# Cross-attention and quantised FFN on one core: the loads of the first batch's tokens and context issued by ScalarE instead of SyncE

## The chip, the cores and the metric

The kernel runs on one core of one Trainium2 chip. The metric is the device time of one execution in microseconds (us), the median of the runs made. Engines are named as the profile names them: PE (TensorE matmul), PEld (its weight loads), DVE (VectorE), ACT (ScalarE), POOL (GpSimd) and SP (SyncE). SP computes nothing: it issues DMAs, and "SPq" in a profile line is SP at work on an issue.

## The reference

For 8 batches of 512 tokens of width 512, a layer norm of the tokens attends to 64 context rows per batch, the result is added to the tokens, and a feed-forward layer with quantised activations and ternary weights (hidden width 2048) is added to that. Cut to what matters:

```python
def xattn(xn, mem, mask):                       # xn = layernorm(x)
    scores = einsum('bsd,bmd->bsm', xn, mem) / sqrt(D)
    attn = softmax(where(mask[:, None, :], scores, -1e30))
    return where(any(mask), einsum('bsm,bmd->bsd', attn, mem), 0)

def linear_bit(x, w, g):
    xq = act_quant(rmsnorm(x, g))               # 8 bits, one scale per row
    wq = round(tanh(w / mean(abs(w)))) * arctanh(mean(abs(w)))
    return einsum('bsd,od->bso', xq, wq)

x = x + xattn(layernorm(x), ctx, mask)
y = layernorm(x)
x = x + linear_bit(silu(linear_bit(y, w1, g1)) * linear_bit(y, w2, g2), w3, g3)
```

Each of the three weight matrices is 4 MB. Its quantisation needs the mean of its absolute values first, so all of a matrix has to be in the chip before any of it can be used.

## The kernel before

All work is recorded as operations (`op(engine, cost, run, writes, reads)`) and then emitted in an order that is stored in the kernel as a packed list, `ORDER`. The costs given to `op` are those of a planner that made the list; the list is fixed, and the costs are not read when the kernel is built. Each engine does its own instructions in the order in which they were emitted, and waits where an operand is not there yet. SP issues every DMA of this kernel in the same way, one after the other. Eight semaphores tell of the landings of DMAs and are used in turn, so the issue of a DMA also waits until the DMA eight places before it in the order has landed.

The tokens of a batch are one tile `x` of 128 partitions, 4 rows of 512 numbers each (`c` = 0 to 3); the context of a batch is loaded twice into one tile `mem`, into partitions 0 to 63 and 64 to 127, 128 KB each. For two batches at a time the context also goes into a tile `both`, from which only a power-of-two scale per batch is taken. `load_x(b)` records these loads: `both` (L473, even batches only), two halves of `mem` (L478), and `x` (L485), which for batch 0 comes in two pieces of 512 KB (`c` = 0 and 1, then 2 and 3) and for the others in one of 1024 KB. `load_w(i)` records four loads of 1024 KB of a weight matrix (L322 and L326, tile `raw`).

The order of the first DMAs on SP is: the mask (L276, 64 KB), `both` (256 KB), the first half of `mem`, the first piece of `x`, the second half of `mem`, the second piece of `x`, then the four pieces of the first weight matrix, and then gains and further weights.

What the first loads feed, each on its engine in this order:

- DVE: unpacks the mask (`keep`, L281); takes the largest number of each row of `both` (`measure_mem`, L494), then of the columns after a transpose on PE (L502), limits and rounds it (L506, L513), and after a broadcast on PE (L517) makes the scales (L519 to L524, tile `mf`). Then come statistics of the first two rows of `x` (L560, L562), the low part of the split context (`split_mem`, L536, which reads `mem`, `mf` and ACT's high part), statistics of the other two rows of `x` (L560, L562) and shifts (L573).
- ACT: a load of its function table, the high part of the split context (L533, reads `mem` and `mf`), a copy (L310), one normalised row of `x` (L582), and then sums of absolute weights (`measure_w`, L353, reads `raw`), one line for each piece of the matrix.
- POOL: variances and inverse roots of them (L567, L291), normalised rows (`t`, L586), their low parts (`xh`, L592), later one half and more of the quantisation of weights (`tq`, L386).

After some 80 us all three weight matrices are quantised and transposed, and the matmuls of the eight batches run one after the other on PE to the end.

Of the kernel before, what the change touches and what calls it, by code (L numbers as in the profile page):

```python
# [59 lines left out]
PE, DVE, ACT, POOL, DMA = "PE", "DVE", "ACT", "POOL", "DMA"  # L60
# [27 lines left out]
class Plan:  # L88
# [19 lines left out]
    def op(self, engine, cost, run, writes, reads, table=None, other=()):  # L108

        me = len(self.ops)
        deps = set()
        pair = lambda x: x if isinstance(x, tuple) else (x, None)
        meets = lambda a, b: a is None or b is None or a == b
        for b, part in map(pair, reads):
            deps.update(o for q, o in b.writes if meets(part, q))
            b.reads.append((part, me))
            b.ops.append(me)
        for b, part in map(pair, writes):  # L120
            deps.update(o for q, o in b.writes + b.reads if meets(part, q) and o != me)
            b.writes.append((part, me))
            b.ops.append(me)
        tiles = {id(b): b for b, _ in map(pair, [*writes, *reads])}.values()
        self.ops.append(Op([(engine, cost, run), *other], deps, [b for b in tiles if b.tag], table))
        return me
# [72 lines left out]
def kernel(  # L199
# [15 lines left out]
    M = mem.shape[1]  # L215
    H = w1.shape[0]
    NC = S // P
# [16 lines left out]
    V, A, G, T, Q = nc.vector, nc.scalar, nc.gpsimd, nc.tensor, nc.sync  # L234
    plan = Plan()
    op = plan.op
# [4 lines left out]
    def few(name, n, key, dtype=F32, bufs=6):  # L241
        return plan.buffer(small, name, [P, n], dtype, bufs, f"{name}_{key}", bound=False)
# [226 lines left out]
    def load_x(b):  # L469
        if b % 2 == 0:  # L470
            both = plan.buffer(att, "both", [P, D], F32, BOTH, f"both_{b}")
            op(DMA, (475, 650, 729),
               lambda: Q.dma_start(both(), mem[b : b + 2].rearrange("b m d -> (b m) d")), [both], [])  # L473
            mem_f[b] = mem_f[b + 1] = measure_mem(b, both)
        mt = plan.buffer(att, "mem", [P, D], F32, 2, f"mem_{b}")
        for half in range(2):
            op(DMA, (475, 650, 364, 500),
               lambda half=half: Q.dma_start(mt()[half * M : (half + 1) * M, :], mem[b]),  # L478
               [(mt, half)], [])
        xt = plan.buffer(big, "big", [P, NC, D], F32, BIG, f"x_{b}")  # L480
        view = x[b].rearrange("(p c) d -> p c d", c=NC)
        n = 2 if b == 0 else NC
        for c in range(0, NC, n):
            op(DMA, (475, 650, 2750 * n // NC, 1400),
               lambda c=c: Q.dma_start(xt()[:, c : c + n, :], view[:, c : c + n, :]),  # L485
               [(xt, c + i) for i in range(n)], [])
        mts[b], xs[b] = mt, xt

    def measure_mem(b, both):


        f = few("mf", 7, b)
        op(DVE, 673,
           lambda: V.tensor_reduce(  # L494
               f()[:, 0:1], both(), AX.X, ALU.max, apply_absolute_value=True), [(f, 0)], [both])
        pr = plan.buffer(ps_a, "a", [1, 2, M], F32, 1, f"pam_{b}")
        op(PE, 110,
           lambda: T.transpose(pr().rearrange("p b m -> p (b m)"), f()[:, 0:1], ident()),
           [pr], [(f, 0), ident])
        tops = few("top", 2, b, bufs=2)  # L500
        top = lambda: tops()[0:1, :]
        op(DVE, 270, lambda: V.tensor_reduce(top(), pr(), AX.X, ALU.max), [tops], [pr])  # L502
        def limit():
            for i in range(2):
                one = tops()[0:1, i : i + 1]
                V.tensor_scalar(one, one, 2e-38, None, ALU.max)  # L506

        op(DVE, 209, limit, [tops], [])

        def power():  # L510
            for i in range(2):
                one = tops()[0:1, i : i + 1].bitcast(I32)
                V.tensor_scalar(one, one, 0x7F800000, None, ALU.bitwise_and)  # L513

        op(DVE, 209, power, [tops], [])
        pe = plan.buffer(ps_a, "a", [P, 2], F32, 1, f"pe_{b}")
        op(PE, 110, lambda: T.matmul(pe(), ones(), top(), start=True, stop=True),  # L517
           [pe], [ones, tops])
        op(DVE, 150, lambda: V.reciprocal(f()[:, 1:3], pe()), [(f, 1)], [pe])  # L519
        op(DVE, 150,  # L520
           lambda: V.tensor_scalar(f()[:, 3:5], pe(), float(D) ** -0.5, None, ALU.mult),
           [(f, 2)], [pe])
        op(DVE, 70,
           lambda: V.tensor_tensor(f()[:, 5:7], pe(), valid()[:, b : b + 2], ALU.mult),  # L524
           [(f, 3)], [pe, valid])
        return f
# [487 lines left out]
    constants()  # L1014
    masks()
    load_x(0)
    load_w(0)
    for g, src in enumerate((g1, g2)):
# [11 lines left out]
    for c in range(AHEAD):  # L1030
        for j in range(NW):
            gate(0, c, j)
    whole(quantise_w(1))
    load_x(1)
    load_w(2)
    whole(measure_w(2))
# [16 lines left out]
    def during(b):  # L1053

        t = 4 * NC * b
        if b == 0:
            job(t, t + 3, quantise_w(2))
            job(t + 0, t + 4, pre(1), expo(1))
            job(t + 5, t + 6, post(1))
            z = quantise_x(1)  # L1060
            job(t + 7, t + 11, half(z)), job(t + 12, t + 15, half(z))
            job(t + 6, t + 6, once(load_x, 2))
            job(t + 10, t + 10, once(load_x, 3))
            job(t + 12, t + 15, pre(2))
            return
        if b + 1 < B:
            z = quantise_x(b + 1)
            job(t, t + 3, expo(b + 1), post(b + 1))
            job(t + 4, t + 7, half(z)), job(t + 12, t + 15, half(z))
        if b + 2 < B:  # L1070
            job(t + 8, t + 15, pre(b + 2))
        if b + 3 < B:
            job(t + 3, t + 3, once(load_x, b + 3))
# [70 lines left out]
```

## Time and profile before

| what | value |
|---|---|
| median of 3 runs | 428.0 us (427.61 to 428.92) |
| the profiled execution | 427.9 us, of which its span is 425.8 us |
| busy, share of the span | PE 91%, DVE 87%, POOL 87%, ACT 80% |
| PE busy, 0 to 80 us | 47.7 us |
| PE busy, 110 to 420 us | 309.8 of 310 us |
| DMA queue of the program | one (q1), 66.93 MB |

A line of the profile's groups gives the source line, the engine, the operation, what it writes and reads, and a count. A line of the timeline gives start and duration in us, the engine (SPq for SP's issues), the source line, the operation, `out<-in`, and in square brackets how long the engine sat idle before it and what ended that. "DMA to landing" is the time from the start of an issue until the semaphore told that all bytes had arrived. The view by stretches gives, for each stretch, its length, the busy time of each engine with the number of instructions, the granted clock of PE, the mean busy share of the 16 DMA engines and the rate of the data.

### The profile page before, as it was taken

How to read it: one execution, taken by the hardware profiler on the slowest of the kernel's cores; microseconds unless marked ns; L12 is line 12 of the kernel's file. 1: busy time of each engine (PE TensorE's matmuls, PEld its weight loads, DVE VectorE, ACT ScalarE, POOL GpSimd, SP SyncE). 2: the span in 40 equal slices, each digit the busy share in tenths (PEclk: the TensorE clock that was granted, in tenths of full speed). 3: DMA queues.
4: the chain of work that ended last, by engine and by line, in shares of the span. 5: the costliest groups of instructions: out<-in, count | busy, mean ns of one | idle time of the engine just before them, and what ended most of it. 6: DMA issues, size and time to landing. Idle time of an engine off the chain costs nothing.

```text
span 425.8 us, 6677 instructions
## 1 busy us (share of the span) xinstructions
PE 388.8 (91%) x2174; PEld 192.8 (45%) x2174; DVE 369.0 (87%) x832; ACT 341.3 (80%) x464; POOL 368.7 (87%) x330
## 2 busy tenths in 40 slices
PE   0563878999999999999999999999999999999996
PEld 0341534544444544454445444544454444444444
DVE  4689999999998998799989998999789888897772
ACT  1799999979899799598996898988686986774531
POOL 1789998998999999699999999999699979988650
PEclk9996899999999999999999999999999999999999
DMA  7999994497555578863589635864644546533272
GB/s 217 408 406 376 380 208 52 103 255 147 126 112 150 99 131 157 183 174 68 104 158 276 136 76 82 171 174 83 134 76 148 75 87 146 152 77 73 49 207 90
DMA packets 142514, 67.35 MB, mean 158 GB/s; under 512 B 133136, under 2 KB 133520, under 8 KB 140048
## 3 DMA queue, kind: packets, MB, share of 16 engines
q1 hardware_dynamic: 142480, 66.93, 63.4%
q8 instruction: 17, 0.28, 0.3%
q14 instruction: 17, 0.14, 0.1%
HBM read 25.76 MB, written 8.39 MB: 80 GB/s over the span
## 4 chain that ended last, share of the span: by engine, by line
PE 78%; DVE 6%; POOL 6%; DMA 3%; issue 3%; ACT 2%; SPq 0%; DVEq 0%; POOLq 0%; ACTq 0%
PE p L883 48%; PE pd L825 24%; PE po L683 3%; DMA zT<-xm 2%; PE psc L602 2%; POOL tq L386 2%; DVE st L560 1%; DMA both<-in_ctx_dram 1%; PE pd L854 1%; POOL t L586 1%; POOL xh L592 1%; POOL mv L291 1%; DVE zf L741 1%; DVE h L927 1%; ACT h L899 1%
## 5 line engine op out<-in xcount | busy, mean ns | idle before, releaser
L883 PEld LDWEIGHTS <-zT 128*128 128x128 f16 x1024 | 99.5, 98 | 122.0 <-issue 3.0
L940 POOL TENSOR_TENSOR h<-h,g_bc 128x1024 f32<-128x1024 f32 x55 | 130.4, 2377 | 2.7 <-ACT sq L932 2.1
L883 PE MATMUL p<-w1T,zT 128*128 128x512 f16 x512 | 120.4, 383 | 2.4 <-DVE zT L309 1.5
L883 PE MATMUL p<-w2T,zT 128*128 128x512 f16 x512 | 119.2, 379 | 1.1 <-DVE h L927 0.9
L825 PE MATMUL pd<-w3T,hT 128*128 128x512 f16 x496 | 117.8, 379 | 0.0
L927 DVE SCALAR_TENSOR_TENSOR h<-p,zf,h 128x1024 f32<-128x1024 f32 x64 | 81.9, 1280 | 14.9 <-PE p L883 8.4
L899 ACT ACTIVATE h<-p,zf 128x1024 f32<-128x1024 f32 x64 | 70.1, 1105 | 24.8 <-PE p L883 17.0
L932 ACT ACTIVATE sq<-h 128x1024 f16<-128x1024 f32 x64 | 67.2, 1050 | 17.0 <-DVE h L927 14.8
L825 PEld LDWEIGHTS <-hT 128*128 128x128 f16 x496 | 47.9, 98 | 55.6 <-DMA hT<-h 0.2
L964 DVE TENSOR_REDUCE hf<-h 128x1 f32<-128x2048 f32 x31 | 70.6, 2278 | 1.8 <-POOL h L940 1.7
L736 POOL TENSOR_TENSOR z<-xm,g_bc 128x1024 f32<-128x1024 f32 x29 | 69.8, 2423 | 1.4 <-ACT xm L725 0.6
L997 ACT ACTIVATE h<-h,hf 128x2048 f16<-128x2048 f32 x23 | 45.8, 1994 | 0.2 <-DVE hf L968 0.2
L741 DVE TENSOR_REDUCE zf<-z 128x2 f32<-128x1024 f32 x32 | 38.8, 1211 | 5.8 <-POOL z L736 5.7
L592 POOL TENSOR_TENSOR xh<-t,xh 128x512 f16<-128x512 f32 x32 | 37.3, 1168 | 2.0 <-DVE xh L591 1.2
L799 ACT ACTIVATE xm<-z,zf 128x512 f16<-128x512 f32 x42 | 28.1, 709 | 0.7 <-DVE zf L760 0.7
L731 ACT ACTIVATE xsq<-x,xf 128x512 f32<-128x512 f32 x32 | 22.9, 715 | 6.5 <-DVE x L691 6.0
L835 DVE SCALAR_TENSOR_TENSOR x<-pd,hf,x 128x512 f32<-128x512 f32 x31 | 23.1, 744 | 3.0 <-PE pd L825 2.6
L691 DVE SCALAR_TENSOR_TENSOR x<-po,mx,x 128x512 f32<-128x512 f32 x32 | 22.9, 745 | 1.3 <-PE po L683 1.2
L602 PE MATMUL psc<-mT,xT 128*128 128x128 f16 x256 | 19.7, 224 | 1.9 <-DMA xT<-xh 1.9
L560 DVE BATCH_NORM_STATS2 st<-x 128x6 f32<-128x512 f32 x32 | 21.3, 679 | 0.0
L602 PEld LDWEIGHTS <-xT 128*128 128x128 f16 x256 | 16.9, 101 | 8.5 <-DMA xT<-xh 3.5
L291 POOL TENSOR_TENSOR hf<-hf,neg_half 128x1 f32<-128x1 f32 x32 | 20.1, 634 | 0.2
(134 smaller groups left out, 483.4 us busy)
## 6 DMA issues: line engine op xcount, KB each, us to landing
raw<-in_L_ffn_w_dram SPq DMA_DIRECT2D x10, 1024.0 KB, 13.8
x<-in_x_dram SPq DMA_DIRECT2D x7, 1024.0 KB, 6.9
out_dram<-x SPq DMA_DIRECT2D x7, 1024.0 KB, 4.1
mem<-in_ctx_dram SPq DMA_DIRECT2D x16, 128.0 KB, 6.5
w3T<-in_L_ffn_w_dram SPq DMA_DIRECT2D x2, 1024.0 KB, 12.6
both<-in_ctx_dram SPq DMA_DIRECT2D x4, 256.0 KB, 8.2
x<-in_x_dram SPq DMA_DIRECT2D x2, 512.0 KB, 6.1
g_bc<-in_L_ffn_g_dram SPq DMA_DIRECT2D x1, 1024.0 KB, 14.9
```

Source lines behind the costliest of these rows:

```text
L592: rest = lambda e, t=t, xh=xh: e.tensor_tensor(xh()[:, 1, :], t(), xh()[:, 0, :], ALU.subtract)
L602: T.matmul(psc()[:, c, :, :].rearrange("p s m -> p (s m)"), xT()[:, k, :], mT().rearrange("p (s d) m -> p d s m", s=2)[:, k % ND, :, :], s ...
L736: gain = lambda e, xm=xm, z=z: e.tensor_tensor(z(), xm().broadcast_to([P, 2, D]), g_bc(), ALU.mult)
L741: lambda i=i, z=z, am=am: V.tensor_reduce(am()[:, i, :], z(), AX.X, ALU.max, apply_absolute_value=True),
L825: T.matmul(po(), hT()[:, n * P : (n + 1) * P], w3T()[:, n, :], start=(n == 0), stop=(n == NH - 1),)
L883: T.matmul(ps()[:, k * HC : (k + 1) * HC], zT()[:, g * ND + d, :], weight(d, j * HW // HC + k), start=(d == 0), stop=(d == ND - 1),)
L899: lambda: A.activation(h()[:, j * HW : (j + 1) * HW], ps(), AF.Silu, scale=fac()[:, 0:1]),
L927: lambda: V.scalar_tensor_tensor(cols(), ps(), fac()[:, 1:2], cols(), ALU.mult, ALU.mult),
L932: lambda: A.activation(sq(), cols(), AF.Square, scale=(RMS / H) ** 0.5, accum_out=col(j)),
L940: run = lambda e: e.tensor_tensor(cols(), cols(), g3_bc()[:, j * HW : (j + 1) * HW], ALU.mult)
L964: lambda: V.tensor_reduce(col(2), h(), AX.X, ALU.max, apply_absolute_value=True),
L997: op(ACT, 1995, lambda: A.activation(hq(), h(), AF.Copy, scale=col(5)), [h], [(f, 5)], other=[(POOL, 1970, lambda: G.tensor_scalar(hq(), h ...
```

## The change

In `load_x`, for batch 0 alone, the four loads of `mem` and `x` are issued by `nc.scalar` (`A`, ACT) instead of `nc.sync` (`Q`, SP). The load of `both` stays on SP, and so do all loads of other batches. The stored order is the same, so SP goes from `both` straight to the first weight piece, and ACT's first four instructions are the two halves of `mem` and the two pieces of `x`, in the order that they had. The changed planner costs (60 for 475) have no effect on the stored order.

```diff
+        queue = A if b == 0 else Q
         mt = plan.buffer(att, "mem", [P, D], F32, 2, f"mem_{b}")
         for half in range(2):
-            op(DMA, (475, 650, 364, 500),
-               lambda half=half: Q.dma_start(mt()[half * M : (half + 1) * M, :], mem[b]),
+            op(DMA, (60 if b == 0 else 475, 650, 364, 500),
+               lambda half=half: queue.dma_start(mt()[half * M : (half + 1) * M, :], mem[b]),
                [(mt, half)], [])
...
         for c in range(0, NC, n):
-            op(DMA, (475, 650, 2750 * n // NC, 1400),
-               lambda c=c: Q.dma_start(xt()[:, c : c + n, :], view[:, c : c + n, :]),
+            op(DMA, (60 if b == 0 else 475, 650, 2750 * n // NC, 1400),
+               lambda c=c: queue.dma_start(xt()[:, c : c + n, :], view[:, c : c + n, :]),
                [(xt, c + i) for i in range(n)], [])
```

## The prediction

> **What bounds the kernel now.** I read the page first: PE is busy 91% of the span. The view by stretches then says where PE is not the bound: from 110 to 420 us it is busy 309.8 of 310 us, from 0 to 80 us only 47.7 of 80. After 80 us the time is PE's own, so the change can only move the moment at which PE's steady stretch begins. Next come the stretches of the start:
>
> ```profile
> core 0: us, PE busy (x) PEld busy (x) DVE busy (x) ACT busy (x) POOL busy (x), PEclk, DMA share, GB/s
> 0.00:2.00 2.00, 0.00 (x0) 0.00 (x0) 0.54 (x4) 0.00 (x0) 0.69 (x6) 1.00 0.02 6
> 2.00:4.00 2.00, 0.00 (x0) 0.00 (x0) 0.05 (x1) 0.00 (x0) 0.00 (x0) 1.00 0.50 174
> 4.00:6.00 2.00, 0.04 (x1) 0.07 (x1) 1.25 (x3) 0.00 (x0) 0.00 (x0) 1.00 1.02 250
> 6.00:8.00 2.00, 0.85 (x3) 0.51 (x3) 1.30 (x7) 0.00 (x0) 0.00 (x0) 1.00 0.98 252
> 8.00:10.00 2.00, 0.04 (x1) 0.00 (x0) 1.70 (x7) 1.45 (x2) 0.13 (x1) 1.00 0.97 340
> 10.00:12.00 2.00, 0.78 (x8) 0.46 (x8) 1.42 (x3) 0.73 (x2) 0.79 (x2) 1.00 1.05 408
> ```
>
> The DMA engines are half idle from 2 to 4 us, and fully busy at only 250 GB/s while `x` and `mem` arrive, against 408 GB/s with weights. In the order of time the chain that ended last begins with the load of `both` (1.18 to 5.11 us), then DVE's work on it, then POOL. The timelines show who waits:
>
> ```profile
> 1.18 0.42 SPq L473 DMA_DIRECT2D both<-in_ctx_dram  x1
> 1.64 0.56 SPq L478 DMA_DIRECT2D mem<-in_ctx_dram  x1
> 2.24 0.57 SPq L485 DMA_DIRECT2D x<-in_x_dram  x1
> 2.86 0.47 SPq L478 DMA_DIRECT2D mem<-in_ctx_dram  x1
> 3.38 0.59 SPq L485 DMA_DIRECT2D x<-in_x_dram  x1
> 4.00 5.33 SPq L322 DMA_DIRECT2D raw<-in_L_ffn_w_dram  x4
> ...
> 8.53 1.28 ACT L533 ACT_TABLE_LOAD   x1 [8.53 <-DMA mem<-in_ctx_dram]
> 9.83 0.72 ACT L533 ACTIVATE ms<-mem,mf 128x512 f16<-128x512 f32 x1
> ...
> 8.22 0.15 DVE L524 TENSOR_TENSOR mf<-pe,valid 128x2 f32<-128x2 f32 x1
> 8.29 1.28 DVE L560 BATCH_NORM_STATS2 st<-x 128x6 f32<-128x512 f32 x2
> 9.48 0.30 DVE L562 BATCH_NORM_AGGREGATE mv<-st 128x2 f32<-128x6 f32 x2
> 10.58 0.75 DVE L536 SCALAR_TENSOR_TENSOR ms<-mem,mf,ms 128x512 f16<-128x512 f32 x1 [0.80 <-ACT ms L533]
> 11.25 1.28 DVE L560 BATCH_NORM_STATS2 st<-x 128x6 f32<-128x512 f32 x2
> ...
> 13.02 0.19 POOL L567 TENSOR_SCALAR mv<-mv 128x2 f32<-128x2 f32 x1 [2.14 <-DVE mv L562]
> ```
>
> To be seen: ACT's table load waits for `mem` alone (in the trace the wait for its two halves stands ahead of it; the scale `mf`, ready at 8.25 us, is waited for only by the ACTIVATE behind it). Those 1.28 us come after the landing of `mem`, then ACT's 0.72 us, and DVE sits 0.80 us for it. POOL waits 2.14 us for DVE's second statistics. So the start has two chains: `both` to DVE, and the second half of `mem` to ACT to DVE. Landings, from the issues of these tiles: `mem` takes 3.9 and 5.6 us, so its halves land at 5.5 and 8.4; `x` 5.8 and 6.5, so at 8.0 and 9.8; the first weight piece 8.4, at 12.4.
>
> **The change part by part.** *Four issues leave SP.* They take 0.56 + 0.57 + 0.47 + 0.59 = 2.19 us; the first weight piece is issued at 1.64 instead of 4.00. The third and fourth pieces still wait, by the semaphores used in turn, for the mask (ready for DVE at 3.95) and `both`. *Four issues join ACT.* No row shows ACT issuing; taken at SP's durations with SP's gaps of 0.05 us, and begun at 0.72 like SP's first, they end near 3.1. ACT's first other work stands at 8.53, so 5.4 us cover them; at twice the price they would still end at 5.4. Cost 0; without cover, 2.2.
>
> *`mem` and `x` are issued 0.9 to 1.0 us earlier* (`mem` at 0.72 and 1.94, `x` at 1.3 and 2.5), into the half idle stretch. But weights now run beside them. If the two queues take turns row by row, the four loads (1280 KB) share with as many bytes of weights and `both`: 1.31 MB at half of 250 to 408 GB/s is 6.4 to 10.5 us, at two thirds (rows of `x` are 4 KB, of weights 2 KB) 4.8 to 7.9, begun near 2 us. The second half of `mem` ends after 60% of the bytes; 60% of these spans from 2 us on is 4.9 to 8.3, and I take 7.2 us for its landing; the last of `x` has bounds of 6.8 and 12.5, and I take 9.8, its time now.
>
> *The gain at ACT.* With `mem` at 7.2 the table load runs 7.3 to 8.6, partly under DVE's scale work, and ACT's high part starts at 8.6, ends at 9.3. DVE comes free at 9.72 (the end of L562 less the overlap of 0.06 us that its rows show), so L536 starts there, not at 10.58: -0.86 us. Any landing of `mem` before 7.6 gives the whole of it (1.28 + 0.72 + 0.1 us before 9.72); at 8.4 nothing. The last of `x` must then be there by 10.39 (11.25 less 0.86); 9.8 is.
>
> *The cost at `both`.* It stays on SP, issued at 1.18, but `mem` and `x` are now in flight beside it. Sharing equally, its 256 KB let 256 KB of others past: 1.0 us at 250 GB/s, of which half an idle DMA stretch pays 0.5. I take +0.5 us on its landing. Bounds: 0, if the idle half of 2 to 4 us takes all; +1.6, if 640 KB (`mem` and a piece of `x`) pass it at 250 GB/s (2.6 us) less the 1.0 us idle. Behind it are queued in order L494, L287, L284, L502 to L524, and then L560: DVE's whole start moves by it, ACT and POOL after it. With +0.5, DVE is free at 10.2, L536 starts there: the net gain of the two is 0.36.
>
> *Weights earlier.* The idle 1.0 us of 2 to 4 us can be filled once, so weights land up to 1.0 us earlier, more if mixed rows run better than 250 GB/s. ACT's waits for weights today are 0.25 (17.60) and 0.52 us (20.12). They are not on the chain, which runs there on POOL (L586, L592); earlier weights only keep ACT from becoming late next, as it would if the chain moved 0.36 and the weights did not. Downstream two waits are for transfers queued behind weights: DVE for the second `both`, 0.27 us at 42.59, and ACT for a transposed tile, 0.66 us at 61.62. With the other engines 91 to 100% busy from 30 to 60 us I count 0.2 of these 0.93 as gained; bounds 0 and 0.93.
>
> Sum against the profiled execution: 427.9 - 0.86 + 0.5 - 0.2 = 427.3 us. That execution is 0.1 under the median of 428.0; its span is 425.8, with 2.1 outside it that the change doesn't touch. A measurement of this kernel can tell about 0.3%, 1.3 us, from no change, so the forecast is no change that can be told.
>
> *Two rules weighed.* The row: four issues take 2.19 us of SP, and 250 GB/s is the rate with one queue. The Trainium skill, page "DMA: Bandwidth & Descriptors", section "Issuing engines are not separate DMA queues", says that all issuers feed the same 16 engines and that a second issuer saves only the issue time; by it nothing is gained in rate, weights lead by 1.0 us at most, and the sum stays 427.3. The same page, section "Queues, rings and completion order", says that engines change between queues only after a packet, of typically 9 to 17 descriptors. No row of this case has two such queues at once. By that rule two weight packets of some 16 rows would pass ahead of the last of `x`, an estimate of 1.05 MB, 2.6 us at 408 GB/s, less the 1.0 us idle: it would land at 11.4, DVE's gain would be gone, and the time would be 427.9.
>
> **The rivals.** *Faster: `both` isn't delayed.* For it: the DMA engines are half idle while it runs. Against: `both` would pass with 1280 KB on another queue beside it. Then -0.86, and with the lead in weights -0.27 and -0.66: 426.1; with half of the latter, 426.6.
>
> *Slower: the weights overtake `x`.* SP hands over two weight pieces before ACT has issued its last load. If transfers are served whole, in the order of issue, those 2.1 MB pass at 408 GB/s ahead of the last of `x`: 5.1 us, less up to 1.0 of earlier start, and it lands near 14.3. DVE's statistics then start 3.05 us later than at 11.25, and POOL with them: 431.0. It decides from a landing after 11.25, and goes beyond the measurable from 12.5. Against: ACT, free from 0.7 us on, has issued its last load by 3.1, when SP has issued two weight pieces and no more; and if the queues take turns, the sharing above gives 9.8.
>
> *Slower: `both` waits for ACT's whole queue.* 1280 KB at 250 GB/s are 5.2 us, less 1.0 idle, and 0.86 gained by `mem`: +3.4, 431.3. Two fifths of it already crosses the bound.
>
> *Nothing moves.* If what generates DMAs serves SP and ACT one after the other, loads leave in nearly the old order: 427.9.
>
> **How the numbers follow.** Forecast 0.30, nothing moves 0.08: 0.38 within the bound. Faster 0.28. Weights overtake 0.22, `both` waits 0.12: slower 0.34. The forecast's own range is 426.5 (no delay of `both`, 0.5 gained downstream) to 428.6 (delay 1.6, nothing downstream). Signs on both sides hold the chance, so the range goes from 426.2, just above the far end of the faster case, to 430.3, some two thirds of the slower ones' price.
>
> **What would show it.** Right: ACT's table load starts near 7.3 us and no longer ends the wait of DVE at L536; L494 starts near 5.6; L560's second pair near 10.9 without a wait; POOL's second L567 near 12.7; the first L353 has no wait; PE's steady stretch begins 0.4 to 0.7 us earlier. Wrong: L494 starts after 6.5, or L560's second pair waits for `x`, or ACT's issues take over 1.5 us each.

## The result, and the profile after

The changed kernel takes 430.37 us (median; 429.32 to 431.36) against 428.81 us for the kernel before measured with it (427.61 to 429.39). The ratio is 1.0037, 95% interval 1.0019 to 1.0054: 1.6 us slower, outside what a measurement takes for no change and 0.1 us above the predicted range. The kernel before is itself 0.8 us above the 428.0 us that the prediction started from, and 1.6 us on top of that would lie inside the range; what was wrong is the direction, a gain of 0.7 us forecast and a loss of 1.6 us measured. The profiled execution is 429.8 us with a span of 427.7 us, 1.9 us more than before in both.

The queues on the page (packets, MB, share of 16 engines) show that the edit did what it says, and so does the list of DMA issues (KB each, median us from issue to landing): `x` goes by ACT's queue, q10.

```profile
q1 hardware_dynamic: 142032, 65.62, 62.1%
q10 hardware_dynamic: 448, 1.31, 1.0%
...
x<-in_x_dram ACTq DMA_DIRECT2D x2, 512.0 KB, 8.2
```

The stretches of the start, after:

```profile
2.00:4.00 2.00, 0.00 (x0) 0.00 (x0) 0.00 (x0) 0.00 (x0) 0.00 (x0) 1.00 0.44 103
4.00:6.00 2.00, 0.00 (x0) 0.00 (x0) 0.48 (x2) 0.00 (x0) 0.00 (x0) 1.00 1.05 332
6.00:8.00 2.00, 0.37 (x1) 0.08 (x1) 1.97 (x7) 0.00 (x0) 0.00 (x0) 1.00 0.90 260
8.00:10.00 2.00, 0.56 (x2) 0.50 (x2) 1.26 (x7) 0.00 (x0) 0.00 (x0) 1.00 1.06 301
10.00:12.00 2.00, 0.00 (x0) 0.00 (x0) 0.60 (x3) 1.74 (x2) 0.92 (x2) 1.00 1.03 404
```

The half idle stretch from 2 to 4 us, into which the loads were to move, carries less than before: 103 GB/s for 174. From 4 us on the engines are as full as they were, at 260 to 332 GB/s, and over the first 10 us the bytes are about the same (the rates times 2 us give 2.0 MB in both). So against this profile a second queue won nothing in rate. Against a second profile of the kernel before, shown below, which moves 2.4 MB in its first 10 us, it lost. The order in which the bytes went has changed as well. The timelines show which bytes paid (line numbers from L475 on are one higher than before):

```profile
0.72 0.56 ACTq L479 DMA_DIRECT2D mem<-in_ctx_dram  x1
1.31 0.60 ACTq L486 DMA_DIRECT2D x<-in_x_dram  x1
1.95 0.52 ACTq L479 DMA_DIRECT2D mem<-in_ctx_dram  x1
2.50 1.07 ACTq L486 DMA_DIRECT2D x<-in_x_dram  x1
10.25 1.28 ACT L534 ACT_TABLE_LOAD   x1 [10.25 <-DMA mem<-in_ctx_dram]
11.55 0.72 ACT L534 ACTIVATE ms<-mem,mf 128x512 f16<-128x512 f32 x1
...
4.85 0.43 DVE L281 CAST keep<-mask_u 128x512 f32<-128x512 uint8 x1 [3.30 <-DMA mask_u<-in_mask_BxS_bk_dram]
5.95 0.69 DVE L495 TENSOR_REDUCE mf<-both 128x1 f32<-128x512 f32 x1 [0.67 <-DMA both<-in_ctx_dram]
9.11 1.27 DVE L561 BATCH_NORM_STATS2 st<-x 128x6 f32<-128x512 f32 x2
10.30 0.30 DVE L563 BATCH_NORM_AGGREGATE mv<-st 128x2 f32<-128x6 f32 x2
12.30 0.75 DVE L537 SCALAR_TENSOR_TENSOR ms<-mem,mf,ms 128x512 f16<-128x512 f32 x1 [1.70 <-ACT ms L534]
12.97 1.28 DVE L561 BATCH_NORM_STATS2 st<-x 128x6 f32<-128x512 f32 x2
...
14.73 0.19 POOL L568 TENSOR_SCALAR mv<-mv 128x2 f32<-128x2 f32 x1 [3.04 <-DVE mv L563]
```

ACT's table load still waits for `mem`, and `mem` is complete at 10.16 us instead of 8.44: +1.72. From there one step hangs on the next: table load 10.25, high part 11.55, DVE's low part 12.30 (+1.72), DVE's second statistics 12.97 (+1.72), POOL 14.73 (+1.71). Compared instruction by instruction, POOL is 1.71 us later at 20 us, 1.71 at 100 us and 1.89 at 420 us; what was lost in the first 10 us is not won back. The landing times of the first loads (us; `mem` and `x` by halves, then the first weight piece):

| kernel | mask | `both` | `mem` | `x` | weights | DVE's second statistics |
|---|---|---|---|---|---|---|
| before | 3.93 | 5.10 | 5.52, 8.44 | 8.05, 9.83 | 12.40 | 11.25 |
| after | 4.83 | 5.92 | 5.35, 10.16 | 8.17, 11.95 | 12.88 | 12.97 |

The trace records each row as it is moved, with its queue, its size and the time it starts. Counting the rows started before the second half of `mem` is complete gives where it was held up:

| started by then, KB | mask and `both` | `mem` | `x`, first piece | `x`, second piece | weights | sum |
|---|---|---|---|---|---|---|
| before, 8.44 us | 320 | 256 | 512 | 360 | 0 | 1448 |
| after, 10.16 us | 320 | 256 | 512 | 324 | 604 | 2016 |

The 568 KB more are weights (604 KB, less 36 KB of `x`), which now run on SP's queue beside ACT's. Over the 1.72 us that is 338 GB/s, a rate of the size of these stretches.

The weights themselves land 0.5 us late, but none of ACT's first four sums of weights (15.18 to 20.86 us in the changed kernel) waits for them, so their landing is not what makes this stretch late.

### The profile page after: what moved, and what is told of

Read it like the earlier page. It is cut to its first block, busy times and chain, and to the rows that moved or that the text cites. A ratio compares the mean times of both kernels' runs of the same rounds, so it can differ in the third digit from the quotient of the medians.

```text
span 427.7 us, 6678 instructions
## 1 busy us (share of the span) xinstructions
PE 392.1 (92%) x2174; PEld 195.0 (46%) x2174; DVE 367.1 (86%) x832; ACT 341.1 (80%) x464; POOL 368.9 (86%) x330
## 4 chain that ended last, share of the span: by engine, by line
PE 80%; DVE 8%; POOL 4%; DMA 3%; issue 3%; ACT 1%; SPq 0%; DVEq 0%; POOLq 0%
PE p L884 48%; PE pd L826 23%; PE po L684 3%; PE psc L603 2%; DMA zT<-xm 2%; PE pw L396 2%; DVE st L561 1%; DMA both<-in_ctx_dram 1%; POOL tq L386 1%; DVE h L928 1%; PE pd L855 1%; DVE at_f L434 1%; POOL xh L593 1%; POOL mv L291 1%; DVE w1T L390 1%
## 5 line engine op out<-in xcount | busy, mean ns | idle before, releaser
L884 PE MATMUL p<-w1T,zT 128*128 128x512 f16 x512 | 121.7, 386 | 2.3 <-DVE zT L309 1.5
L928 DVE SCALAR_TENSOR_TENSOR h<-p,zf,h 128x1024 f32<-128x1024 f32 x64 | 81.9, 1280 | 17.1 <-PE p L884 8.4
```

The lines of the kernel that those rows point to most:

```text
L884: T.matmul(ps()[:, k * HC : (k + 1) * HC], zT()[:, g * ND + d, :], weight(d, j * HW // HC + k), start=(d == 0), stop=(d == ND - 1),)
L928: lambda: V.scalar_tensor_tensor(cols(), ps(), fac()[:, 1:2], cols(), ALU.mult, ALU.mult),
```

## The experiments

The theory after this, A in the expectations: `mem`'s second half stands behind a piece of `x` in ACT's queue, while SP's queue passes on weights beside it; DVE and POOL follow through ACT's table load. The rivals: the loss comes from `both` and the mask, which share the start with ACT's queue (B); or ACT's queue is slow in itself. Behind each expectation stands the ratio of the run's time to that of the kernel before, with its 95% interval.

**The order in ACT's queue.** Meant was `mem`, `mem`, `x`, `x` by issuing both halves where the first was recorded:

```diff
-               lambda half=half: queue.dma_start(mt()[half * M : (half + 1) * M, :], mem[b]),
+               lambda half=half: [queue.dma_start(mt()[k * M : (k + 1) * M, :], mem[b])
+                                  for k in ((half,) if b else (0, 1) if half == 0 else ())],
```

> Changed kernel, but ACT issues both halves of mem ahead of x. Theory A (the second half of mem, behind a piece of x in ACT's queue and beside weights, holds ACT's table load and all behind it): mem has landed by 6.5 us (10.2 in the changed kernel), the table load runs under DVE's work, ACT's L533 starts near 9.1 (11.6), DVE's second pair of statistics waits for x alone and starts near 12.0 (13.0), and about 0.9 of the 1.6 us come back: +0.7 us on the kernel before. Theory B (the loss is the later landing of the mask and of both, 0.8 to 0.9 us, and what ACT waits for is swallowed later): no change, +1.6.

The stored order takes the other half first, so the queue became `x`, `mem`, `mem`, `x`, and the run tells something else than was meant. 1.0066 (1.0047 to 1.0085), the slowest of all. The timelines of SP's issues, ACT and DVE:

```profile
0.72 0.40 SPq L276 DMA_DIRECT2D mask_u<-in_mask_BxS_bk_dram  x1
...
0.72 0.41 ACTq L487 DMA_DIRECT2D x<-in_x_dram  x1
...
11.15 1.28 ACT L535 ACT_TABLE_LOAD   x1 [11.15 <-DMA mem<-in_ctx_dram]
...
6.57 0.43 DVE L281 CAST keep<-mask_u 128x512 f32<-128x512 uint8 x1 [5.01 <-DMA mask_u<-in_mask_BxS_bk_dram]
8.67 0.69 DVE L496 TENSOR_REDUCE mf<-both 128x1 f32<-128x512 f32 x1 [1.68 <-DMA both<-in_ctx_dram]
```

The mask is issued at 0.72 us as always, but with a piece of `x` beside it it lands 2.6 us later than before, and `both` 3.5 us later. The 14 rows of `x` that start from 2 to 3 us here take 436 ns on average. In the changed kernel, where the first rows of `x` start at 4.09 us, the 12 up to 4.5 us take 159 ns, and in the kernel before those from 4.0 to 4.5 us take 390 ns. What makes rows of the same 4 KB slow is not shown.

The order that was meant, by `(1, 0) if half == 1`:

> Changed kernel, with ACT's order mem, mem, x, x (in e1 a piece of x went first, since the stored order takes the later half of mem first; here both halves do). Theory A (mem and x late behind each other and beside weights; a shift of the start reaches the end whole): both halves land by 6.5 us, L533 starts near 9.1 when DVE has its scale, the last of x lands near 12 as in the changed kernel and DVE's second pair starts there: +0.8 to +1.1 us on the kernel before. Theory B2 (a piece of x at the head of ACT's queue is what holds up mask and both): with 256 KB of mem ahead of x, mask and both land no later than in the changed kernel, 4.8 and 5.9. If they land later still, by 0.5, it is the bytes ahead, whatever tile they belong to.

1.0040 (1.0026 to 1.0054), as slow as the change. `mem` is complete at 7.63 us, earlier than before, and yet DVE's second statistics start at 12.76:

```profile
7.72 1.28 ACT L535 ACT_TABLE_LOAD   x1 [7.72 <-DMA mem<-in_ctx_dram]
10.04 0.72 ACT L535 ACTIVATE ms<-mem,mf 128x512 f16<-128x512 f32 x1 [1.04 <-DVE mf L521]
...
6.89 0.69 DVE L496 TENSOR_REDUCE mf<-both 128x1 f32<-128x512 f32 x1 [1.04 <-DMA both<-in_ctx_dram]
10.64 1.29 DVE L562 BATCH_NORM_STATS2 st<-x 128x6 f32<-128x512 f32 x2 [0.51 <-DMA x<-in_x_dram]
```

Now ACT waits for DVE's scale, because `both` lands at 6.87, and DVE for the first piece of `x`, which lands at 10.62 with weights beside it. So the wait for `mem` can be taken away, but another of the same size stands behind it. The mask and `both` land later than in the changed kernel (5.40 and 6.87 us for 4.83 and 5.92) with 256 KB of `mem` at the head of ACT's queue for 128 KB, and later still in the run before it with 512 KB of `x` there (6.54 and 8.65): by the rule set in the expectation it is the bytes at the head of the other queue that hold them up, whichever tile they belong to.

**Weights held back.** On the changed kernel, a write of one number into the first weight tile after the mask's unpacking keeps SP's first weight issue from 1.64 until 5.32 us:

```diff
-        op(DVE2, 470, lambda: V.tensor_copy(keep(), mask_u8()), [keep], [mask_u8])
+        def unpack():
+            V.tensor_copy(keep(), mask_u8())
+            V.memset(raw[0, 0]()[0:1, 0:1], 0.0)
+
+        op(DVE2, 470, unpack, [keep], [mask_u8])
```

> Changed kernel, but the first weight piece is held back on SP until DVE has unpacked the mask (a one-element memset of its tile by DVE, about 4.9 us instead of 1.6). Theory A with the weights as the cause: the second half of mem lands by 8.2 and the last of x by 9.8, DVE's second pair starts near 11.3, and the time is that of the kernel before, +0.0 to +0.3 us, though mask and both stay 0.8 us late (they share with mem and x, not with weights). If ACT's queue itself is the slower one, mem stays near 10 and the time near +1.6. Theory C (weights that land 0.5 us late set the time): worse than +1.6, since weights land later still.

```profile
5.32 3.95 SPq L326 DMA_DIRECT2D raw<-in_L_ffn_w_dram  x4
...
9.23 1.28 ACT L538 ACT_TABLE_LOAD   x1 [9.23 <-DMA mem<-in_ctx_dram]
...
4.84 0.43 DVE L282 CAST keep<-mask_u 128x512 f32<-128x512 uint8 x1 [3.29 <-DMA mask_u<-in_mask_BxS_bk_dram]
...
11.28 0.75 DVE L541 SCALAR_TENSOR_TENSOR ms<-mem,mf,ms 128x512 f16<-128x512 f32 x1 [0.35 <-ACT ms L538]
...
166.06 1.90 PE L888 MATMUL p<-w2T,zT 128*128 128x512 f16 x8 [0.81 <-DMA zT<-xm]
```

The trace answers for the theory in part: `mem` lands 1.02 us earlier than in the changed kernel, DVE's wait for ACT falls from 1.70 to 0.35 us, and its second statistics start at 11.96 instead of 12.97. The mask is still late (4.82 us) and `both` even more so (6.25), so these two lose to `mem` and `x`, not to weights. The time did not follow, and the expectation of +0.0 to +0.3 us is a miss: 1.0048 (1.0032 to 1.0065). Against the kernel before, POOL is 0.7 us late at 20 us and 1.0 from 25 us on, but 1.9 at 180 us and 2.6 from 250 us on. Part of what is lost far behind the edit stands in PE's timeline: 0.81 us of waiting at 166.06 us for a tile whose transpose by DMA took 4.68 us to land, where it took 3.44 in the kernel before, and 0.62 us at 234.38 us for another. The kernel before and the changed kernel show no wait of PE over 0.2 us there. Why that transpose took longer, and whether it does in every execution, is open. So a part of the theory is shown by the landings, and not by the time.

**The table load moved to the front.** A small activation right behind the `x` loads makes ACT load its table while it has nothing else to do; on the changed kernel and, with `Q.dma_start`, on the kernel before:

```diff
-               lambda c=c: queue.dma_start(xt()[:, c : c + n, :], view[:, c : c + n, :]),
+               lambda c=c: [
+                   queue.dma_start(xt()[:, c : c + n, :], view[:, c : c + n, :]),
+                   b == 0 and c and A.activation(g3_bc()[0:1, 0:P], ones(), AF.Copy, scale=1.0)],
```

> Changed kernel, with ACT's table load taken off the path: behind its last issue ACT runs a 1x128 copy into a tile that nothing has used yet, so the table is loaded at about 3.6 us. Theory A: ACT's L533 starts when mem lands, 10.3 instead of 11.6, DVE's L536 near 11.0, and its second pair near 12.0, where x now ends the wait: +0.6 us on the kernel before. Theory B: no change, +1.6.

1.0030 (1.0015 to 1.0046). On the timelines of this kernel:

```profile
3.64 1.28 ACT L488 ACT_TABLE_LOAD   x1 [3.64 <-issue]
10.36 0.72 ACT L536 ACTIVATE ms<-mem,mf 128x512 f16<-128x512 f32 x1 [5.12 <-DMA mem<-in_ctx_dram]
...
11.12 0.75 DVE L539 SCALAR_TENSOR_TENSOR ms<-mem,mf,ms 128x512 f16<-128x512 f32 x1 [0.50 <-ACT ms L536]
12.09 1.29 DVE L563 BATCH_NORM_STATS2 st<-x 128x6 f32<-128x512 f32 x2 [0.22 <-DMA x<-in_x_dram]
```

Of the 1.28 us, 0.88 come back at DVE's second statistics (12.09 for 12.97); then the last piece of `x`, complete at 12.07 us, is what is waited for. The loads arrive too late, table or no table. The time lies 1.3 us above the kernel before, more than the +0.6 expected; in the profiled execution POOL is 0.9 us late at 20 us and 2.7 at 180 us, and PE waits 1.12 us at 166.79 us for the same transpose as with the weights held, which took 4.99 us here.

> Kernel before, with the table load taken off the path in the same way (behind the last load of x in program order; ACT has nothing else then). Theory A: L533 starts at 8.6 instead of 9.8, DVE's L536 follows at 9.7 without a wait, its second pair at 10.4, and 0.8 us are gained: -0.8 us on the kernel before. If a shift of the start is swallowed before PE's steady stretch: 0.

0.9988 (0.9977 to 0.9998), a gain below what can be told. DVE's second statistics start at 10.26 instead of 11.25; but in the second profile of the kernel before they start at 10.59 without any edit, so at most some 0.3 us of this can be put down to the table load. POOL is 1.0 us earlier at 20 us but 0.74 from 25 us on. ACT's waits for weights (0.33 and 0.57 us) are hardly longer than before (0.25 and 0.52). What grew is DVE's wait for PE at L366, from 0.23 to 0.48 us, in stretches where PE's granted clock is 0.56 (22 to 24 us) and 0.59 (24 to 26 us), against 1.00 in the kernel before.

**One part of the change alone.** `mem` on ACT, `x` back on SP:

> Changed kernel with x back on SP: ACT issues only the two halves of mem, SP mask, both, x, x and then weights. Weights no longer run beside x. Theory A: mem lands by 6.0, x at 8.0 and 9.8; if ACT's mem alone makes mask and both 0.8 us late, DVE's whole start is 0.8 late and the gain of 0.86 at its wait for ACT goes on that: 0.0 (-0.2 to +0.2). If mask and both are late by x in ACT's queue, not by mem, they land at 4.2 and 5.4 here, and -0.5.

1.0024 (1.0012 to 1.0037), slower than either of the two outcomes expected. Both halves are issued from 0.72 us on, and `mem` is complete at 7.72, but `both`, with `mem` beside it, lands at 6.78:

```profile
4.98 0.43 DVE L281 CAST keep<-mask_u 128x512 f32<-128x512 uint8 x1 [3.43 <-DMA mask_u<-in_mask_BxS_bk_dram]
6.80 0.69 DVE L495 TENSOR_REDUCE mf<-both 128x1 f32<-128x512 f32 x1 [1.39 <-DMA both<-in_ctx_dram]
```

DVE's first statistics move by that (9.96 for 8.29), and its second come at 12.06. So half of the change is enough to be slower, by the other of the two chains.

Only `both` on ACT, `mem` and `x` on SP, an edit of one line on the kernel before (`(A if b == 0 else Q).dma_start(both(), ...)`):

> Kernel before, with only the first load of both issued by ACT, beside the mask; SP's loads of mem and x start 0.46 us earlier. If two queues beside each other cost what the changed kernel shows (mask +0.9), the mask lands near 4.8 and DVE, which takes it first, starts 0.3 late although both lands near 5.0; mem's second half near 8.0: between -0.3 and +0.3. If the cost is that of x and mem alone, mask at 4.0 and both at 4.6: -0.4.

0.9992 (0.9977 to 1.0007), no change. `both` lands at 5.12, where it did; the mask, which now runs beside it, at 4.73 instead of 3.93, still in time for it. With the early table load in addition:

> Kernel before with ACT issuing the first load of both and then loading its table (both edits of e8 and e7 together). If the two gains add: -0.3 and -0.5 give -0.8 us on the kernel before, L533 near 8.2, DVE's second pair near 10.3. If the weights' landing (19.2 in both of them) is what the start then waits for, no more than e7 alone: -0.5.

0.9983 (0.9969 to 0.9998), no more than the table load alone.

**The same new order on one queue.** On the kernel before, SP issues `mem`, `mem`, `x`, `x`:

> Kernel before with the order mask, both, mem, mem, x, x on SP: one queue as before, but neither half of mem stands behind x. Theory A: both halves land by 6.2, the table load goes under DVE's work, x lands 0.3 later at most in its first piece, DVE's second pair starts near 10.4 instead of 11.3, and as with the table load moved 0.6 to 0.8 us are gained: -0.7. If x in its first piece (8.0 now, used at 8.3) slips beyond 8.6, the gain falls by that.

1.0025 (1.0010 to 1.0040), a miss. `mem` lands at 6.34 us and the table load is out of the way at 7.72, but the first piece of `x` slips to 8.82 (DVE waits 0.35 for it) and the weights to 12.89. POOL is 0.3 us early at 20 us and 2.0 late at 90 us; ACT waits 0.78, 0.55 and 0.54 us for the weights. Why these land later, with the same bytes before them, is open. PE's granted clock was lower as well in this execution, 0.50 from 24 to 28 us where the kernel before has 1.00; how much of the loss belongs to which is not shown.

**All six loads on ACT's queue, none beside them.** On the changed kernel the mask and `both` go to ACT too, and the write that held the weights back above holds SP's weights until 4.45 us:

> Changed kernel with mask and both on ACT too, and weights held on SP until the mask is unpacked: the six first loads stand in ACT's queue alone, in the old order, and weights come no earlier than in the kernel before. If it is the sharing of two queues that makes the start late (theory A), mask lands at 3.9, both at 5.1, mem at 5.5 and 8.4, x at 8.0 and 9.8, and the time is that of the kernel before: 0.0 (-0.3 to +0.4). If a queue of ACT's is slower than SP's, mask and both are late as in the changed kernel, and +0.8 or more.

```profile
1.62 0.53 ACTq L483 DMA_DIRECT2D mem<-in_ctx_dram  x1
2.19 0.59 ACTq L490 DMA_DIRECT2D x<-in_x_dram  x1
2.82 0.47 ACTq L483 DMA_DIRECT2D mem<-in_ctx_dram  x1
3.32 0.61 ACTq L490 DMA_DIRECT2D x<-in_x_dram  x1
...
7.93 1.28 ACT L538 ACT_TABLE_LOAD   x1 [7.93 <-DMA mem<-in_ctx_dram]
...
3.97 0.43 DVE L282 CAST keep<-mask_u 128x512 f32<-128x512 uint8 x1 [2.42 <-DMA mask_u<-in_mask_BxS_bk_dram]
5.08 0.69 DVE L499 TENSOR_REDUCE mf<-both 128x1 f32<-128x512 f32 x1 [0.68 <-DMA both<-in_ctx_dram]
```

This settles the last rival. On ACT's queue alone the six loads land at 3.95, 5.06, 5.57, 7.09, 7.84 and 9.53 us, within the two profiles of the kernel before or ahead of them, and the issues take what they took on SP. ACT's queue is not slow. Weights were held back in the earlier run too, which took 430.46 us; what differs here is that the mask and `both` no longer stand on another queue than `mem` and `x`. So the loss comes with the two queues at work on these loads at once. It does not come with every use of two queues: with only `both` on ACT nothing but the mask was late. The time is 427.52 us against 428.47, 0.9977 (0.9965 to 0.9990), the fastest kernel of all here, though by less than the 0.3% that were taken as the least to be told. Where this 1.0 us comes from is not shown: the weights are issued 0.45 us later than before, and but for `both`, by 0.04 us, the first loads land no earlier than in the better of the two profiles of the kernel before (the second of them is shown next).

**The two kernels looked at again,** one execution each:

> Kernel before, unchanged, profiled once more beside the other runs: how far one execution's landings differ from another's. If they are those of the load order alone, x lands at 8.0 and 9.8 and the first weight piece at 12.4 again, each within 0.2; in e7, with the same loads, they came 1.0 earlier (7.0, 8.9, 11.4), so I expect a spread of about 1 us in the first piece of x and in all that lands after it, and 0.1 in mask and both.

> Changed kernel, unchanged, profiled once more. Theory A expects the same picture within that spread: mask 4.8, both 5.9, mem's second half near 10 and the last of x near 12, DVE's second pair near 13. If mem's second half lands before 8.5 here, the first profile was an accident and the cause is elsewhere.

427.12 us (span 424.9) and 429.87 us (427.8), both on one chip; the record does not say which chip the first two profiles came from. The changed kernel repeats itself: `mem` at 10.31, DVE's second statistics at 13.12. The kernel before does not: the same loads in the same order bring `mem` at 7.78 and `x` at 7.01 and 9.26, each 0.6 to 1.0 us earlier than in the profile that the prediction was made from. In its timeline the wait of DVE for ACT is gone, without any change, and its stretches from 4 us on move more than the 250, 252 and 340 GB/s of the first profile:

```profile
9.92 0.75 DVE L536 SCALAR_TENSOR_TENSOR ms<-mem,mf,ms 128x512 f16<-128x512 f32 x1
10.59 1.28 DVE L560 BATCH_NORM_STATS2 st<-x 128x6 f32<-128x512 f32 x2
...
4.00:6.00 2.00, 0.00 (x0) 0.00 (x0) 1.12 (x3) 0.00 (x0) 0.00 (x0) 1.00 1.03 324
6.00:8.00 2.00, 0.71 (x3) 0.46 (x3) 1.47 (x7) 0.13 (x1) 0.00 (x0) 1.00 1.01 299
8.00:10.00 2.00, 0.27 (x3) 0.19 (x4) 1.75 (x8) 1.87 (x2) 0.00 (x0) 1.00 1.03 396
```

So the 250 GB/s that the prediction worked with were those of one execution. The changed kernel moves 2.0 MB in its first 10 us in both profiles, the kernel before 2.0 and 2.4 MB.

## Why the prediction was wrong

*The step that failed: the landing of `mem`'s second half.* It was taken at 7.2 us, with bounds of 4.9 and 8.3; it is 10.16 and 10.31. The prediction had the sharing right: of the bytes started by 10.16 us, 1092 KB are ACT's and 924 KB SP's, near to halves. The rate was at the low end of its bounds: 60% of the four loads' bytes had started by 8.32 us, about the upper bound, so some 1.1 of the 3.0 us are the choice of 7.2 within the range. The other 1.8 us are what was wrong in "the second half of `mem` ends after 60% of the bytes". That holds if the 16 DMA engines keep in step and a load has landed as soon as its last row has started. Neither is so here: the rows of the second half start from 7.18 to 9.19 us, and the landing is told 0.97 us after the last of them, by 16 signals that come from 8.47 to 10.16 us. By then 1092 of 1280 KB, 85%, have started, most of the piece of `x` behind it among them. The trace of before had this in it: there the 16 signals come from 6.89 to 8.44 us, and at 8.44 us 1128 of the same 1280 KB had started, 88%. With 85% in the place of 60%, the prediction's own spans (4.8 to 10.5 us, from 2 us on) give 6.1 to 10.9 us. Then the gain of 0.86 would have been one end of a range, with a loss of up to some 2.5 us (10.9 for 8.44) at the other.

*The gain at ACT, -0.86, became +1.72.* Every step of the chain was named rightly, and its sign was set by the landing alone. The prediction said that a landing at 8.4 gains nothing; a landing later than that had no price. With the scale ready at 9.2 and statistics done at 10.54 (10.30 + 0.30 less the 0.06 overlap), DVE would have started L537 where it did before, at 10.58, even with `both` late, if `mem` had landed at 8.44. So `mem` ends the wait that costs 1.72. Not all of it would have come back without that wait: the last of `x`, taken at 9.8, lands at 11.95 and would have held the second statistics 0.7 us beyond 11.25, as it does in the run with the early table load (12.09). Besides, the second look at the kernel before shows that the 0.86 was not there to be had in every execution: its DVE did not wait.

*The cost at `both`, +0.5, was +0.82,* within its bounds. The mask, which DVE needs first, was left out: it lands 0.90 later (4.83). Neither is what ended last in the changed kernel, but both are what makes the version with `mem` alone on ACT slower in its first 12 us.

*Weights earlier, -0.2, was nothing.* They were issued 2.4 us earlier and landed 0.48 later (12.88). "The idle 1.0 us of 2 to 4 us can be filled once" fell: 340 KB started there before, 201 and 247 KB in the two looks at the changed kernel. Downstream of 20 us the shift stays at 1.71 up to 100 us, so nothing of the 0.93 us was found there.

*Issues on ACT* cost nothing, as said: 0.52 to 1.07 us each, over by 3.57.

*The rivals.* "The weights overtake `x`" (431.0) had the right cause, weights that pass beside ACT's queue, and the right sign, but looked at the wrong tile. The last of `x` lands at 11.95, beyond its deciding point of 11.25, and still ends no wait, because DVE is not there before 12.97. "`both` waits for ACT's whole queue" asked for +4.2 at `both`; it was +0.82. "`both` isn't delayed" and "nothing moves" fell. None of the three signs named as "wrong" showed (L494 after 6.5, a wait for `x`, long issues). It was the signs named as "right" that failed: the table load at 10.25 for 7.3, a wait of 1.70 at L537 for none, the second pair at 12.97 for 10.9, POOL at 14.73 for 12.7.

*The two rules.* The Trainium skill, page "DMA: Bandwidth & Descriptors", section "Issuing engines are not separate DMA queues", says that a second issuer saves issue time only; the stretches of 103, 332, 260 and 301 GB/s agree that no rate is won, and they show a loss in the first (174 and 168 in the two profiles of the kernel before), of which the section says nothing. Of packets of 9 to 17 descriptors, which the section "Queues, rings and completion order" gives as the step at which engines change between queues, the runs decide nothing. In the run with both halves of `mem` first, from 8.0 to 10.5 us, 177 rows of weights and 167 rows of `x` start, near one for one; turns of one row and turns of equal packets both look so, as the records don't name the engine.

## What to carry to other kernels

Before loads are split over two queues, find the one whose landing the chain hangs on, and count all bytes that will be started before it, those of the other queue and those behind it in its own: here a load whose place in its queue was 60% was told complete only when 85 to 88% of the queue's bytes had started. A second queue with work from the first issue on took here from what stood first and is small, the mask and the scale's input, and gave the place to what needs it least, the weights. A stall of 0.8 us seen in one execution should be looked for in a second one before it is counted as a gain. And a shift at the start should be followed to the end: with the weights held, 0.7 us at 20 us had become 2.6 us at 250 us.

## What the runs showed of the hardware that was not expected

- Two queues with work from the first issue on moved less in the stretch from 2 to 4 us: 103 and 127 GB/s (the two looks at the change), 106, 114, 123 and 125 (both halves of `mem` first, a piece of `x` first, weights held, `mem` alone on ACT), and 161 to 186 with one queue, on SP or on ACT. With only `both` on ACT it was 212, and 209 with the early table load in addition. Why is open; how many bytes the rows in front hold may play a part.
- ACT's last issue of `x` took 1.07 and 0.91 us in the two looks at the changed kernel, 0.60 with the weights held back, so here an issue became longer while the other queue was being filled; with `mem`, `mem`, `x`, `x` on ACT it took 0.44, weights beside it too.
- ACT's table load stands behind the wait of the first activation (8.53 us for `mem`, 10.25 in the changed kernel); with an activation on data at hand it ran at 3.64 us, and at 0.72 in the kernel before, in idle time.
- With the six loads on ACT's queue, the first row of the weights, issued by SP at 4.45 us on a queue that held nothing else, starts at 7.83 us, when 936 of the 1024 KB of `x` have started; the mask's first row starts 1.03 us after its issue. That looks like service in the order of issue rather than in turns; no run tests it.
- The same six loads on one queue land up to 1.0 us apart from one execution to the next (the first piece of `x` at 8.05 and 7.01 us), and part of it reaches the end: POOL is 0.68 us apart at 20 us and 0.88 at 420 us. Whether that is the execution or the chip is not shown.
